# A transformer block on one core: identity transposes at the start, later weight loads, a sixth lo tile, normalisation ahead of its transposes

## The chip, the core and the metric

The kernel runs on one core of a Trainium2 chip. It is written in Bass with the Tile framework. The metric is device time in microseconds (us) of one execution; lower is better. The engines are TensorE (PE: matmuls and transposes; PEld is its weight load), VectorE (DVE), ScalarE (ACT), GpSimd (POOL) and SyncE (SP, which issues most DMAs). Each engine executes its own instructions in order. The instructions that the kernel pins with `tc.keep_in_program_order` (in the code through `mm`, `transpose` and `act`) stay in the order of the program; the compiler may place the others earlier, by its own estimate of when they are ready. SP's DMAs and ScalarE's normalisations are among these others.

## What is computed

Two sequences of 2048 tokens with 512 features go through one transformer block with adaptive layer norm; 16 heads of 32 features, a hidden layer of 2048, all in float32. The reference, cut:

```python
mod = silu(condition) @ Wada + bada
sh_a, sc_a, gt_a, sh_m, sc_m, gt_m = split(mod, 6, axis=1)
xm = (layernorm(x) * g1 + be1) * (1 + sc_a) + sh_a
q, k, v = split(xm @ Wqkv)                       # heads of 32
scores = causal(q @ k.T * 32 ** -0.5)
x = x + gt_a * (softmax(scores) @ v @ Wproj + bproj)
xm = (layernorm(x) * g2 + be2) * (1 + sc_m) + sh_m
x = x + gt_m * (gelu(xm @ W1 + b1) @ W2 + b2)
```

## The kernel before

The two sequences (rows 0 and 1) go through a QKV stage and an attention stage one after the other: QKV 0, attention 0, projection 0 with the preparation of row 1, QKV 1, attention 1, projection 1, and then one MLP stage for both.

**The opening.** ScalarE's queue loads the small vectors into `rows`. SP loads the first 512 tokens (`load_x(0)`, four tiles of 128 x 512), two 512-column pieces of Wada (`load_wada(0, 1)`, eight DMAs of 256 KB), then the weights of q and k (`load_w`) and of v (`load_wv`). TensorE transposes `rows` into `ps_c` (L1290), from which the column vectors `cols` are copied. For the four token tiles `stats` gives mean and variance on VectorE, and `inv_std` the reciprocal deviation `rstd1` and the `shift1`, with ScalarE's square root between. `norm(0, 0, True)` normalises two tiles on ScalarE (L866) and transposes them with TensorE (`ps_xt`, L212). Then `modulation(0)` multiplies silu(condition) with Wada (`ps_mod`); `norm(0, 1, True)` does the other two tiles; `columns()` adds the bias to `ps_mod` (L1314) and turns the result into columns (`ps_modt`); `scale_shift` makes the factors `a1` and `c1`, and `modulate` writes the modulated, transposed tokens `xmT` from the banks of `ps_xt`.

**A QKV stage** (`Qkv.run`) has four groups of 512 tokens. A group has six units: four of q and k (`keys_and_queries`) and two of v (`values`). A unit is a Strassen product in seven steps of four matmul instructions each, 0.87 us a step. Group 0 of row 0 begins with a plain unit instead (`plain`, L998), which counts as seven steps. After each step `tick` runs, with the step number `n` in the group `g`. It is the schedule that the change edits: at n = 3 the tokens of the next group are loaded, at n = 18 and 28 `norm` does the halves of the next group, statistics first, at 36, 38, 40 the token sums are made, and from n = 7 of group 1 on a plan (`row.count`) inserts score matmuls of the coming attention (`s`), whose maxima VectorE takes (`mx`, L481 and L476). These share two score banks in PSUM (tag "s") with `ps_mod` and `ps_modt`.

**q and k tiles.** The results are gathered in a `lo` tile (five buffers in row 0, six in row 1), rounded into a `hi` tile (three buffers), `lo` becomes the difference, and SP stores both to DRAM (`stored`, L924). A buffer is free again when its store has landed. `key_loads` and `query_loads` bring back what attention needs (L323, L348).

**Prepared weights.** The same stage prepares the MLP weights. `Pieces.plan(f, room, load, start)` loads a piece of W1 or W2 at a tick `load` (SP, L1119 and L1128), adds its Strassen sums on GpSimd from tick `start` on (L1140), and GpSimd's queue stores them to DRAM. Ticks run through the stage: group 0 of row 0 has 41, each further group 42. The rooms are tiles that are not yet in use: parts of the values `vv`, two key tiles and two query tiles (`spare_q`, taken from the four buffers of `qst`). `load_wada(2, 5)` runs at step 7 of group 0, `modulation(g + 1)` at step 10 of groups 1 and 2, `columns()` at step 14, and there `load_wada(3, 4)` in group 1. `mr` holds the bias rows for that in a tile of its own.

**Row 1.** While projection 0 runs, `between(n)` makes the statistics of row 1's first group and runs `norm` at n = 5 and 8. After that QKV 1 is as QKV 0, without Wada and modulation.

## Time and profile before

| | us |
|---|---|
| median of 3 runs (2357.98 to 2359.51) | 2358.91 |
| the profiled execution | 2359.31 |
| its span, first to last instruction | 2357.5 |
| TensorE busy / VectorE / GpSimd / ScalarE | 2311.3 / 1433.9 / 1120.0 / 1008.0 |

TensorE's busy time by stage:

| stretch, us | stage | length | TensorE busy | granted clock |
|---|---|---|---|---|
| 0 to 20 | opening | 20 | 9.25 | 0.98 |
| 20 to 214 | QKV 0 | 194 | 182.92 | 0.98 |
| 214 to 780 | attention 0 | 566 | 561.35 | 1.00 |
| 780 to 816 | projection 0 | 36 | 34.38 | 1.00 |
| 816 to 996 | QKV 1 | 180 | 175.13 | 0.99 |
| 996 to 1560 | attention 1, projection 1 | 564 | 559.30 | 1.00 |
| 1560 to 2357 | MLP | 797 | 788.94 | 1.00 |

How the page is read: a group is a line, an engine, an operation and the tiles it writes and reads; then its count, its busy time and the mean of one instruction, and the idle time of that engine just before, with what ended it. Idle time of an engine that does not set the end costs nothing. Matmuls are pipelined and their ends are modelled, so that a busy TensorE need not be at its peak. The granted clock is the share of full speed that TensorE was given, by the profiler's records; before the first record it is shown as 1.00.

### The profile page before, as it was taken

What the parts mean: (1) busy time and instruction counts of PE and PEld (TensorE: products, weight loads), DVE (VectorE), ACT (ScalarE), POOL (GpSimd) and SP (SyncE); (2) the same over time, 40 slices, a digit from 0 to 9 for tenths busy, and PEclk for the clock granted to TensorE, in tenths of its full rate; (3) what the DMA queues carried; (4) which work ended last, traced back from release to release, by engine and by line L of the source; (5) the groups of instructions that cost most, each with busy time, mean ns of one, the idle gap of its engine ahead of it and who ended that gap; (6) DMA issues with size and microseconds to landing.
All of it is one profiled execution on the core that took longest, in us unless ns stands there. A gap on an engine that the chain in (4) does not pass through costs nothing.

```text
span 2357.5 us, 34284 instructions
## 1 busy us (share of the span) xinstructions
PE 2311.3 (98%) x12033; PEld 1403.5 (60%) x12033; DVE 1433.9 (61%) x2960; ACT 1008.0 (43%) x1952; POOL 1120.0 (48%) x1261
## 2 busy tenths in 40 slices
PE   7999999999999999999999999999999999999998
PEld 5877555555554488855555555444585486487477
DVE  4567666666666666776666666653473374365356
ACT  4434555555555244355555555603323322332321
POOL 7152997978793593289887997460000000000000
PEclk9999999999999999999999999999999999999999
DMA  9887133231232797532324113273254254353433
GB/s 303 262 260 194 38 81 74 64 82 46 79 110 91 256 304 247 140 84 59 82 64 99 38 45 121 78 252 111 94 171 148 89 180 143 115 167 128 135 124 130
DMA packets 160518, 311.64 MB, mean 132 GB/s; under 512 B 16544, under 2 KB 48844, under 8 KB 158552
## 3 DMA queue, kind: packets, MB, share of 16 engines
q1 hardware_dynamic: 155488, 285.53, 40.0%
q0 software_dynamic: 4480, 23.36, 2.6%
q8 instruction: 95, 1.56, 0.3%
q14 instruction: 79, 0.65, 0.1%
q10 hardware_dynamic: 376, 0.55, 0.1%
HBM read 229.95 MB, written 87.29 MB: 135 GB/s over the span
## 4 chain that ended last, share of the span: by engine, by line
PE 92%; DVE 3%; DMA 2%; POOL 1%; ACT 1%; issue 1%; SPq 0%; DVEq 0%; POOLq 0%; ACTq 0%
PE ps_a L204 24%; PE st L204 20%; PE ps_b L204 12%; PE o L204 11%; PE s L204 10%; PE ps_c L204 6%; PE sm L204 4%; PE ps_o L204 3%; PE ps_xt L212 1%; POOL ee L634 1%; DVE mx L481 1%; PE ps_o L212 1%; DVE junk L476 0%; DMA x<-in_x_dram 0%; DMA q<-lo 0%
## 5 line engine op out<-in xcount | busy, mean ns | idle before, releaser
L606 ACT ACTIVATE e<-st 128x512 f32<-128x512 f32 (+1 forms) x1152 | 573.4, 578 | 429.4 <-PE st L204 369.4
L634 POOL TENSOR_TENSOR ee<-ee,e 128x512 f32<-128x512 f32 x424 | 529.3, 1290 | 4.5 <-ACT e L606 4.2
L481 DVE TENSOR_REDUCE mx<-s 128x1 f32<-128x512 f32 x604 | 407.4, 687 | 194.5 <-PE s L204 193.2
L204 PE MATMUL s<-kst,qst 128*128 128x512 f32 (+3 forms) x1032 | 418.6, 409 | 9.3 <-DVE mx L481 7.8
L204 PE MATMUL st<-qst,kst 128*128 128x512 f32 (+3 forms) x1280 | 409.4, 387 | 0.0
L204 PE MATMUL ps_a<-sum,w 128*128 128x256 f32 (+1 forms) x1088 | 346.6, 454 | 0.0
L204 PE MATMUL o<-e,vv 128*32 128x512 f32 (+3 forms) x2560 | 300.5, 538 | 2.0 <-POOL e L612 2.0
L204 PEld LDWEIGHTS st<-qst,kst 128*128 128x128 f32 x1280 | 227.4, 188 | 94.1 <-issue 62.1
L476 DVE CUSTOM_DVE_ANT_0 junk<-s,causal 128x512 bf16<-128x512 f32 (+3 forms) x428 | 208.6, 487 | 106.7 <-PE s L204 99.2
L204 PEld LDWEIGHTS ps_a<-sum,w 128*128 128x128 f32 x1088 | 206.3, 190 | 109.8 <-issue 91.4
L204 PEld LDWEIGHTS s<-kst,qst 128*128 128x128 f32 x1032 | 194.8, 189 | 124.7 <-DVE mx L481 62.0
L634 POOL TENSOR_TENSOR ee<-e 128x512 f32<-128x512 f32 x168 | 210.5, 1287 | 102.3 <-ACT e L606 100.0
L612 POOL TENSOR_SCALAR_AFFINE_SELECT e<-e 128x128 f32<-128x128 f32 (+1 forms) x384 | 122.6, 360 | 82.6 <-ACT e L606 79.8
L204 PE MATMUL st<-fold,sel 32*128 32x512 f32 (+1 forms) x1152 | 148.6, 481 | 0.4
L1590 DVE TENSOR_TENSOR h<-c,ps_b 128x512 f32<-128x512 f32 x32 | 22.0, 687 | 202.4 <-PE ps_b L204 202.4
L204 PEld LDWEIGHTS st<-fold,sel 32*128 32x128 f32 x1152 | 59.1, 181 | 143.1 <-ACT e L606 86.6
L204 PEld LDWEIGHTS o<-e,vv 128*32 128x32 f32 x2560 | 61.3, 108 | 101.8 <-issue 80.1
L204 PE MATMUL ps_b<-sum,w 128*128 128x256 f32 (+1 forms) x384 | 120.6, 450 | 0.0
L1764 ACT ACTIVATE h<-h,cols 128x512 f32<-128x512 f32 x96 | 69.2, 722 | 118.6 <-DVE h L1590 118.6
L481 DVE TENSOR_REDUCE mx<-st 128x1 f32<-128x512 f32 x164 | 112.7, 687 | 4.2 <-PE st L204 2.4
L959 POOL TENSOR_TENSOR lo<-lo,hi 128x512 fp32r<-128x512 f32 x32 | 40.7, 1273 | 134.2 <-ACT hi L957 113.9
L204 PEld LDWEIGHTS ps_b<-sum,w 128*128 128x128 f32 x384 | 73.0, 190 | 37.2 <-issue 30.6
(205 smaller groups left out, 3108.0 us busy)
## 6 DMA issues: line engine op xcount, KB each, us to landing
kst<-k SPq DMA_DIRECT2D x128, 256.0 KB
qst<-q SPq DMA_DIRECT2D x128, 256.0 KB
w<-w1d SPq DMA_DIRECT2D x32, 896.0 KB
w<-w2d SPq DMA_DIRECT2D x28, 1024.0 KB
w<-w2d SPq DMA_DIRECT2D x28, 768.0 KB
q<-hi SPq DMA_DIRECT2D x32, 256.0 KB
q<-lo SPq DMA_DIRECT2D x32, 256.0 KB
k<-hi SPq DMA_DIRECT2D x32, 256.0 KB
```

Of the source, the lines that this page charges most:

```text
L204: return tc.keep_in_program_order(nc.tensor.matmul(*args, **kw))
L212: return tc.keep_in_program_order(nc.tensor.transpose(dst, src, ident[:n, :n]))
L476: nc.vector.tensor_tensor_reduce(junk[:, :w], s[:, :w], causal[:, QB - w :], 1.0, MASKED, ALU.add, ALU.max, m,)
L481: nc.vector.tensor_reduce(m, s[:, :w], axis=AX.X, op=ALU.max)
L606: act(nc.scalar.activation(e[:, :w], sts[h][:, :w], AF.Exp))
L612: nc.gpsimd.affine_select(d, d, pattern=[[0, len(tiles)], [1, P]], compare_op=ALU.is_ge, fill=0.0, base=0, channel_multiplier=-1,)
L634: act(engine.tensor_tensor(dst, x, y, ALU.add))
L959: engine.tensor_tensor(lo, d, hi.bitcast(F32), ALU.subtract)
L1590: act(nc.vector.tensor_tensor(dst, x, y, ALU.add))
L1764: nc.scalar.activation(d, ps, AF.Gelu, bias=col(r_b1 + half * HF + f, 1))
```

## The change

- After the weight loads are issued, TensorE does 34 transposes of the identity into a score bank `ps_w` that nobody reads. They stand ahead of the transpose of `rows`.
- The normalisation leaves `norm` and becomes `normal`. In the opening it runs on VectorE, as (x - mean) * rstd, for all four tiles, and both halves are transposed before `modulation(0)`. In the groups it stays on ScalarE and runs at n = 14 and 24, with the statistics of the group at 14; the transposes stay at 18 and 28. In projection 0 it runs at n = 4 and 7, with the transposes at 5 and 8.
- `lo` has six buffers in both rows. `mr` moves into the end of a spare query tile (the last 512 of 2048 columns; the piece there uses the first 896).
- `load_wada(2, 5)` moves from step 7 to 24 of group 0; `modulation` and `columns` from steps 10 and 14 to 3 and 7 of groups 1 and 2, and with the latter `load_wada(3, 4)`.
- The pieces of W1 and W2 are loaded and summed at later ticks.

```diff
+        def normal(self, g, j, early=False):
+            b = self.row.b
+            if j == 0 and g > b:
+                for t in range(MTT):
+                    self.stats(g, t)
+            for t in (2 * j, 2 * j + 1):
+                n, xt = b * NT + g * MTT + t, self.xts[g][t]
+                if early:
+                    nc.vector.tensor_scalar(
+                        xt, xt, mv1[:, n, 0:1], rstd1[:, n : n + 1],
+                        ALU.subtract, ALU.mult,
+                    )
+                else:
+                    nc.scalar.activation(
+                        xt, xt, AF.Identity,
+                        bias=shift1[:, n : n + 1], scale=rstd1[:, n : n + 1],
+                    )
         def norm(self, g, j, share=False):
             if j == 0:
-                if g > b:
-                    for t in range(MTT):
-                        self.stats(g, t)
                 self.xmT[g] = self.qp.tile([P, C, MT], F32, tag="xmT", ...)
-            for n, xt in enumerate(xts, n0):
-                nc.scalar.activation(
-                    xt, xt, AF.Identity,
-                    bias=shift1[:, n : n + 1], scale=rstd1[:, n : n + 1],
-                )
...
-            return hp.tile([P, MT], F32R, tag="lo", name="lo", bufs=5 + self.row.b)
+            return hp.tile([P, MT], F32R, tag="lo", name="lo", bufs=6)
...
+                        if n in (14, 24):
+                            self.normal(g + 1, n // 24)
                         if n in (18, 28):
                             self.norm(g + 1, n // 28)()
...
+        spare_q = [row.old_queries().rearrange("p h q -> p (h q)") for _ in range(2)]
...
-                mr = wp.tile([P, D], F32, tag="mr", name="mr")
+                mr = spare_q[0][:, HC * QB - D :]
...
+        ps_w = ps_sp.tile([P, QB], F32, tag="s", name="ps_w")
+        for _ in range(34):
+            transpose(ps_w[:, :P], ident)
         ps_c = ps_mm.tile([P, n_rows], F32, tag="mm", name="ps_c")
         transpose(ps_c, rows)
...
-        halves = [qkv.norm(0, 0, True)]
+        for j in range(2):
+            qkv.normal(0, j, True)
+        halves = [qkv.norm(0, j, True) for j in range(2)]
...
         columns = modulation(0)
-        halves.append(qkv.norm(0, 1, True))
         columns()
...
-            if g == 0 and n == 7:
+            if g == 0 and n == 24:
                 load_wada(2, 5)
-            elif g in (1, 2) and n == 10:
+            elif g in (1, 2) and n == 3:
                 qkv.columns = modulation(g + 1)
-            elif g in (1, 2) and n == 14:
+            elif g in (1, 2) and n == 7:
                 qkv.columns()
...
-        pieces.plan(FC // 2, room_2, 5, 17)
+        pieces.plan(FC // 2, room_2, 16, 27)
...
-            (room_v, 4, 38), (room_k, 58, 68), (room_q, 62, 73), (room_k, 84, 93),
-            (room_q, 88, 98), (room_k, 108, 116), (room_q, 112, 121), (room_w, 101, 126),
+            (room_v, 34, 46), (room_k, 64, 73), (room_q, 68, 78), (room_k, 88, 97),
+            (room_q, 93, 102), (room_k, 110, 118), (room_q, 114, 122), (room_w, 104, 126),
...
+            if n in (4, 7):
+                qkv.normal(0, n // 7)
             if n in (5, 8):
                 qkv.norm(0, n // 8)()
```

More of the change, by code (lines that the diff above doesn't have):

```diff
@@ L1381, in dit_block_kernel @@
         pieces = Pieces()
-        spare_q = [row.old_queries().rearrange("p h q -> p (h q)") for _ in range(2)]
         spare_k = [row.key_room(q) for q in (2, 3)]
```

## The prediction

> **What bounds the kernel now.** I read the page first. TensorE is busy 98% of the span and 92% of the chain that ended last, so only what gives TensorE idle time, or a half clock, can move the end. I then asked for the waits of TensorE over the whole span, for stretches of 0.5 and 2 us through the two QKV stages (row 0: 19 to 214 us, row 1: 816 to 995 us), and for the chain and timeline around each idle stretch. The change touches nothing of the attention, projection and MLP matmuls, so the question is how much idle time lies in those stages.

> The opening, from the chain of waits in order of time (start, us, what):

> ```profile
> 8.18 1.53 ACT x L866 x2
> 9.75 1.75 PE ps_xt L212 x7
> 11.51 3.85 PE ps_mod L204 x16
> 15.36 1.24 PE ps_xt L212 x8
> 16.60 0.80 PE ps_modt L204 x8
> 18.12 1.90 DVE xmT L267 x4
> ```

> The first tokens are normalised on ScalarE, eight transposes follow, the modulation matmul `ps_mod`, eight more transposes, the small `ps_modt`, then the modulated tokens; the first projection matmul starts at 19.17. Seven transposes take 1.75 us here (250 ns each), while eight take 0.87 us at 54.92 (109 ns each), and `ps_mod` takes 3.85 us here against 1.86 at 77.48: TensorE runs at half speed, though the clock column shows 1.00 until 19.0.

> The granted clock by stretches (busy us of PE, PEld, DVE, ACT, POOL, then PEclk):

> ```profile
> 19.00:19.50 0.50, 0.33 (x1) 0.33 (x2) 0.50 (x3) 0.50 (x2) 0.48 (x2) 0.69 1.11 352
> 19.50:20.00 0.50, 0.50 (x1) 0.17 (x1) 0.50 (x3) 0.50 (x2) 0.50 (x1) 0.50 1.08 346
> ...
> 22.50:23.00 0.50, 0.50 (x2) 0.19 (x1) 0.50 (x1) 0.00 (x0) 0.50 (x2) 0.89 0.92 324
> ```

> 0.69 and 0.89 put the half-clock stretch at 19.2 to 22.6: 3.4 us, so 1.7 us of TensorE work lost. The 2 us stretches show three more of the same length, at 49.9, 128.4 and 920.3, each just after an idle stretch. So an idle stretch of 2 us or more costs itself and 1.7 us more. The three, from the timeline (start, us, what, in brackets the idle time before and its releaser):

> ```profile
> 33.81 5.21 SPq L1280 DMA_DIRECT2D vv<-in_L_cond_Wada_dram  x8
> 47.51 0.62 ACT L957 CAST hi<-lo 128x512 fp32r<-128x512 f32 x1 [1.89 <-DMA q<-hi]
> 48.68 1.10 PE L204 MATMUL ps_b<-xmT,wqk 128*128 128x256 f32 x4 [3.49 <-ACT lo L952]
> ```

> ```profile
> 116.11 3.92 SPq L1119 DMA_DIRECT2D kst<-in_L_cond_W_dram  x4
> 120.12 2.10 SPq L816 DMA_DIRECT2D x<-in_x_dram  x4
> 124.13 0.69 DVE L216 BATCH_NORM_STATS2 stat<-x 128x6 f32<-128x512 f32 x1 [2.17 <-DMA x<-in_x_dram]
> 127.29 0.44 PE L204 MATMUL s<-kst,qst 128*128 128x384 f32 x1 [1.80 <-DVE mx L481]
> ```

> ```profile
> 872.93 0.33 PE L212 MATMUL ps_xt<-ident,x 128*128 128x128 f32 x1 [0.88 <-ACT x L866]
> ...
> 918.60 0.33 PE L212 MATMUL ps_xt<-ident,x 128*128 128x128 f32 x1 [1.70 <-ACT x L866]
> ```

> First: SP spends 5.2 us issuing Wada, the stores of q queue behind it (the chain has `q<-lo` from 40.64 for 7.49 us), and ScalarE waits for its `hi` and `lo` tiles. Second: the tokens of group 3 are issued behind a W1 load, VectorE waits for them with the score maxima behind it, and one of the two score banks is still held by `ps_mod`. Third: transposes wait for their normalisation.

> **The change, part by part.**

> Opening. The 34 identity transposes can start when the identity is made (1.41+0.29 = 1.70). At 109 ns they end at 5.4, at 250 ns at 10.2. Normalising moves to VectorE and needs no shift: after the reciprocal (7.95) four tensor_scalar of 128x512. The row of that form (L248, in the MLP) is 512 ns at least, 863 median beside GpSimd work; GpSimd is idle from 5.4 to 17.4, so I take 512. First tokens at 8.5, against 9.0; all sixteen transposes end at 10.7 (four per 512 ns). Silu's table load no longer queues between normalisations. `ps_mod` then waits for Wada: its last chunk was waited for until 13.11 (0.57 us behind a DMA), and the load order before it is the same. With the clock up the last quarter takes 0.5 us, end 13.6 against 15.36; the addition 0.69 and eight `ps_modt` at 0.80 follow, then 1.7 us to the first projection as now (17.43 to 19.17): 17.2 against 19.17, **−2.0 us**. Bounds: if the clock stays up through the projection too, 1.7 more (−3.7); if the transposes never raise it, 34 end at 10.2, sixteen more at 250 ns at 14.5 with `ps_c`, `ps_mod` 3.85 at 18.4, first projection at 22.0: +2.8. I take −2.0, with a half-clock stretch after it as now: TensorE still idles about 2 us before the first projection.

> Does an identity transpose count as work for the clock? By the trace, the stretch 2350.5 to 2353.9 holds 0.8 us of matmul and transposes beside it, and the clock stayed at 1.00, while 46.5 to 49.9, with 1.2 us of matmul, was followed by half clock: they seem to count. Against it, 9.0 to 12.4, mostly transposes with TensorE busy for 3.12 of 3.4 us, did not raise it: `ps_mod` ran on at half speed. [...]

> Wada (2,5) from step 7 to 24, the W2 and W1 pieces from 5 and 4 to 16 and 34, and `lo` from five tiles to six. This clears SP and the DMA queue between 26 and 40 us, and the first write of unit 3 meets a tile whose store was issued at 26, not at 40. It removes 3.49 us and the 1.7 after it: **−5.2**. Row 1 has six `lo` tiles and no Wada load, and its first group (816 to 860) shows no such wait. Bounds −5.2 and 0.

> Where does it go? From step 24 to step 14 of group 1 about 26 us pass, which at 390 GB/s (40 to 66 us ran at 390 to 428) carry 10.1 MB. Wada 2.1, W1 0.5, W2/W1 stores 4.0, q/k stores 2.1, tokens 1.0 and, with its load moved from step 14 to 7, the second Wada 2.1 make 11.8: 4 us too much. Late first are the k stores of group 1 behind the second Wada's 5.2 us on SP; their `hi` tile is wanted about 10 steps (8.7 us) later. Bounds 0 and a stall as before, 5.2. I take **+3**, nearer that row, as the sum is over.

> Modulation from steps 10 and 14 to 3 and 7 of groups 1 and 2. Scores run from step 7 on, so `ps_mod` no longer holds a score bank beside them. Tokens are loaded at step 3 and the W1 pieces go from step 1 of group 2 (tick 84) to step 5 (88), so the tokens are ahead of them by 3.92 us of SP. This answers 1.80+0.25+0.48 of idle time and 1.7 of half clock, 4.2; two of its three causes go, I take **−3.1**, bounds −4.2 and 0.

> `normal` at steps 14 and 24 ahead of transposes at 18 and 28, with the statistics, in both rows; in the projection one step ahead. Four steps are 3.5 us or more; the waits are 0.88+0.38 in one group of row 1 and 1.70+0.38+1.7 in another: **−5.1**, bounds −5.1 and 0. No instruction is added; ScalarE (9 of 20 us busy there) and VectorE (14 of 20) hold it. What queues behind: an unfinished token load now meets VectorE and ScalarE four steps sooner, with maxima and `lo` evictions behind. Issue to last statistics is 71.70 to 79.9, 8.2 us; steps 3 to 14 give 11 x 0.87 = 9.6. The cover is 1.4 us.

> At nothing: `mr` in the spare query tile (same memset and wait on GpSimd), the later W1 sums (GpSimd is 48% busy), one more table load wait at 28 to 31 us as now.

> Sum: −2.0 −5.2 +3.0 −3.1 −5.1 = −12.4. The profiled execution took 2359.3 (span 2357.5); the runs' median is 2358.9. So **2347 us**.

> **The rivals.** (a) The warm-up does not do what it says: opening +2.8 in place of −2.0, 2359.3−7.6 = 2351.7. For: the half speed at 9 to 12 us with transposes running. Against: the stretch at the end. (b) The moved transfers stall group 1 of row 0 in place of group 0: +5.2 in place of +3 and the group 3 tokens still late (0 for −3.1): −2.0−5.2+5.2−5.1 = −7.1, 2352; with one of row 1's two waits kept, 2355 or more. For: the 11.8 MB. Against: only stores with slack are late. (c) Slower: tokens land after step 14, in-order VectorE and ScalarE stop there, and each such group costs what group 3 costs now, 4.2. The gains at 128, 872 and 918 fall, −4.2 remains. Six groups have the moved step; from two late groups on the change loses, with three it is −4.2+12.6 = +8.4, 2367.7. For: 1.4 us of cover and a full queue. Against: after the token load at 903.72 the DMA share is 0.82 to 0.88, not full.

> **How the numbers follow.** Forecast 0.53, (a) 0.22, (b) 0.15, (c) 0.10. All bounds at their good end give −19.1, 2340; 2359 leaves out (c) and little else. 0.2% (4.7 us) is what a measurement can tell. Faster: 0.53 + 0.20 of (a) + 0.05 of (b) = 0.78; same: 0.02+0.10 = 0.12; slower 0.10. Without (b)'s poor half and (c) the range would be 2340 to 2354.

> **What would show it.** Right: first projection matmul near 17; transposes of tokens near 109 ns; no wait of `ps_b` for ScalarE near 46; no half clock near 128 and 920; the row 1 stage (815.7 to 995.6 now, 179.9 us) about 5 us shorter. Wrong: token transposes at 250 ns and a first projection after 19 (a); a wait of ScalarE for `q<-hi`, `k<-hi` or `lo` stores between 65 and 90 us (b); VectorE's statistics waiting for `x<-in_x_dram` with TensorE idle in several groups (c).

## The result, and the profile after

The change made the kernel slightly slower: 2363.89 us median of 22 runs against 2359.45 us of 22 runs of the kernel before, a ratio of 1.0018 with a 95% interval of 1.0010 to 1.0026, so 2.4 to 6.1 us. The forecast was 2347, with a range of 2340 to 2359; the result lies above it. The profiled execution of after took 2364.2 (span 2362.5, TensorE busy 2316.3).

How far a mark of after stands from the same mark of before, in the one profiled execution of each, shows the place (us):

| mark | before | after | after less before |
|---|---|---|---|
| first projection matmul | 19.17 | 18.90 | -0.3 |
| first Strassen unit (`ps_a`) | 27.83 | 25.87 | -2.0 |
| attention 0, first matmul | 214.96 | 220.78 | +5.8 |
| QKV 1, first unit | 815.65 | 821.90 | +6.3 |
| attention 1, first matmul | 995.56 | 999.71 | +4.2 |
| MLP, first transposes | 1560.01 | 1564.44 | +4.4 |

So the opening and QKV 1 each gained 2, and QKV 0 lost 7.8 between its first Strassen unit and its end. What TensorE waited for most in the first 215 us of after (in total, times, longest):

```profile
PE ps_a L204 <- POOL wv L846: 8.5, 1, 8.5
PE s L204 <- DVE mx L476: 3.3, 3, 2.7
PE ps_xt L212 <- ACT x L869: 2.0, 2, 1.8
PE ps_a L204 <- DVE lo L982: 1.9, 1, 1.9
```

The wait of `ps_b` for `lo` at 45 to 49 us is gone, as forecast. In its place stands one of 8.5 us. The profile puts it down to GpSimd's value weight sums, but this matmul reads neither `wv` nor anything made from it. The timelines from 23 to 37 us tell more (start, us, what, in brackets the idle time before and its releaser). VectorE of after:

```profile
23.26 0.69 DVE L216 BATCH_NORM_STATS2 stat<-x 128x6 f32<-128x512 f32 x1 [2.92 <-DMA x<-in_x_dram]
26.42 3.08 DVE L1379 COPY pick<-pickc 128x512 f32<-128x512 f32 x1
...
30.69 3.96 DVE L901 TENSOR_TENSOR xmT<-xmT 128x512 f32<-128x512 f32 x1
34.66 0.66 DVE L216 BATCH_NORM_STATS2 stat<-x 128x6 f32<-128x512 f32 x1
```

GpSimd of after:

```profile
26.45 2.77 POOL L841 TENSOR_TENSOR wqk<-wqk 128x256 f32<-128x256 f32 x4
...
30.41 5.37 POOL L846 TENSOR_TENSOR wv<-wv 128x512 f32<-128x512 f32 x4
```

ScalarE and then TensorE of after:

```profile
35.57 0.30 ACT L222 ACTIVATE rstd<-mv,eps 128x4 f32<-128x4 f32 x1 [7.61 <-DVE mv L219]
35.78 0.36 ACT L963 ACTIVATE lo<-ps_a 128x256 f32<-128x256 f32 x1
```

```profile
26.73 1.03 PE L204 MATMUL ps_b<-t,wqk 128*128 128x256 f32 x4
36.24 2.05 PE L204 MATMUL ps_a<-t,wqk 128*128 128x256 f32 x4 [8.48 <-POOL wv L846]
```

Read backwards: TensorE goes on at 36.24, 0.1 us after ScalarE has evicted `ps_a` into `lo`. ScalarE could not evict before, because `rstd` of group 1 stood ahead in its queue and waited 7.61 us for the last mean and variance from VectorE. VectorE was late because it had waited 2.92 us for group 1's tokens ahead of `pick` and `xmT`, a copy and a sum of group 0, and because these two then took 3.08 and 3.96 us beside GpSimd's sums. In before they took 0.94 and 0.84, although they lay beside GpSimd's sums there too. GpSimd, then VectorE of before:

```profile
19.31 10.48 POOL L841 TENSOR_TENSOR wqk<-wqk 128x256 f32<-128x256 f32 x12
```

```profile
24.14 0.94 DVE L1361 COPY pick<-pickc 128x512 f32<-128x512 f32 x1
25.01 0.68 DVE L216 BATCH_NORM_STATS2 stat<-x 128x6 f32<-128x512 f32 x1
...
26.87 0.84 DVE L890 TENSOR_TENSOR xmT<-xmT 128x512 f32<-128x512 f32 x1
```

There GpSimd's sums took 0.87 us each, in after 0.69, so in before it was GpSimd's sums that took longer. What decides which of the two engines takes longer is not shown.

Group 1's statistics are issued at step 14 by the new program text and at 18 by the old one, but in both queues the compiler has placed them near the beginning of group 0. In before they stand behind `pick`; in after the first of them stands ahead of it. By the clock records the clock was at half from 30.6 to 40.9 us; TensorE worked for 4.6 us of that, so 2.3 were lost to it. The windows (busy us of PE, PEld, DVE, ACT, POOL, then PEclk) show both halves of the loss, the idle one and the slow one:

```profile
32.00:36.00 4.00, 0.00 (x0) 0.00 (x0) 3.96 (x5) 0.43 (x2) 3.92 (x4) 0.50 0.56 179
36.50:41.00 4.50, 4.50 (x12) 3.58 (x12) 0.42 (x1) 3.31 (x5) 2.06 (x3) 0.51 0.65 178
```

A second new stretch lies in group 1, where the tokens of group 2 come late. SP, VectorE and TensorE of after:

```profile
77.60 4.35 SPq L816 DMA_DIRECT2D x<-in_x_dram  x4
84.40 6.68 SPq L1294 DMA_DIRECT2D vv<-in_L_cond_Wada_dram  x8
```

```profile
85.33 0.69 DVE L216 BATCH_NORM_STATS2 stat<-x 128x6 f32<-128x512 f32 x1 [6.67 <-DMA x<-in_x_dram]
```

```profile
87.35 0.33 PE L204 MATMUL s<-kst,qst 128*128 128x128 f32 x1 [2.70 <-DVE mx L476]
89.55 3.78 PE L204 MATMUL ps_a<-t,wqk 128*128 128x256 f32 x8 [1.87 <-DVE lo L982]
```

The mechanism is that of rival (c): tokens come late, VectorE stops in order, and score maxima and `lo` stand behind it; that makes 2.70 + 1.87 us idle, and 3.0 us more are lost at half clock from 88.7 to 95.5. The cause is another: the two experiments below that keep the later loads but have the statistics back at step 18 show the same stretch, so the moved loads make it and not the earlier step.

In group 3 VectorE does not wait for its tokens any more, and the score wait of before at 127 us is down to 0.29. In its place TensorE waits for the normalisation, which it did not do there in before, with 3.4 us of half clock as before:

```profile
143.43 0.47 PE L212 MATMUL ps_xt<-ident,x 128*128 128x128 f32 x1 [1.81 <-ACT x L869]
```

### The profile page after: what moved, and what is told of

It reads as the page before. It is cut to its first block, busy times and chain, and to the rows that moved or that the text cites. A ratio compares the mean times of both kernels' runs of the same rounds, so it can differ in the third digit from the quotient of the medians.

```text
span 2362.5 us, 34358 instructions
## 1 busy us (share of the span) xinstructions
PE 2316.3 (98%) x12067; PEld 1409.6 (60%) x12067; DVE 1437.2 (61%) x2964; ACT 1005.3 (43%) x1948; POOL 1117.3 (47%) x1261
## 4 chain that ended last, share of the span: by engine, by line
PE 90%; DVE 3%; DMA 2%; POOL 2%; issue 1%; ACT 1%; SPq 0%; POOLq 0%; DVEq 0%; ACTq 0%
PE ps_a L204 24%; PE st L204 20%; PE ps_b L204 12%; PE o L204 11%; PE s L204 10%; PE ps_c L204 6%; PE sm L204 4%; PE ps_o L204 2%; PE ps_xt L212 1%; DVE mx L481 1%; POOL ee L634 1%; DVE junk L476 1%; PE ps_o L212 1%; DMA x1d<-xt 0%; DMA x<-in_x_dram 0%
## 5 line engine op out<-in xcount | busy, mean ns | idle before, releaser
L481 DVE TENSOR_REDUCE mx<-s 128x1 f32<-128x512 f32 x604 | 407.6, 687 | 196.3 <-PE s L204 195.0
L204 PE MATMUL s<-kst,qst 128*128 128x512 f32 (+3 forms) x1032 | 418.5, 409 | 11.0 <-DVE mx L481 7.1
L204 PE MATMUL st<-qst,kst 128*128 128x512 f32 (+3 forms) x1280 | 409.4, 387 | 0.0
L204 PE MATMUL ps_a<-sum,w 128*128 128x256 f32 (+1 forms) x1088 | 346.6, 454 | 0.0
L204 PE MATMUL o<-e,vv 128*32 128x512 f32 (+3 forms) x2560 | 300.5, 538 | 1.9 <-POOL e L612 1.9
L204 PEld LDWEIGHTS st<-qst,kst 128*128 128x128 f32 x1280 | 227.4, 188 | 94.2 <-issue 62.0
L204 PEld LDWEIGHTS ps_a<-sum,w 128*128 128x128 f32 x1088 | 206.3, 190 | 109.8 <-issue 91.4
L204 PEld LDWEIGHTS s<-kst,qst 128*128 128x128 f32 x1032 | 194.7, 189 | 124.1 <-DVE mx L481 59.3
L204 PE MATMUL st<-fold,sel 32*128 32x512 f32 (+1 forms) x1152 | 148.5, 480 | 0.4
L204 PEld LDWEIGHTS st<-fold,sel 32*128 32x128 f32 x1152 | 59.2, 181 | 143.2 <-ACT e L606 86.6
L204 PEld LDWEIGHTS o<-e,vv 128*32 128x32 f32 x2560 | 61.5, 108 | 101.5 <-issue 79.4
L204 PE MATMUL ps_b<-sum,w 128*128 128x256 f32 (+1 forms) x384 | 120.6, 450 | 0.0
L1783 ACT ACTIVATE h<-h,cols 128x512 f32<-128x512 f32 x96 | 69.3, 722 | 120.4 <-DVE h L1609 120.4
L481 DVE TENSOR_REDUCE mx<-st 128x1 f32<-128x512 f32 x164 | 112.7, 687 | 4.2 <-PE st L204 1.8
L204 PEld LDWEIGHTS ps_b<-sum,w 128*128 128x128 f32 x384 | 73.0, 190 | 37.2 <-issue 30.6
```

The source lines that it names most:

```text
L204: return tc.keep_in_program_order(nc.tensor.matmul(*args, **kw))
L481: nc.vector.tensor_reduce(m, s[:, :w], axis=AX.X, op=ALU.max)
L1783: nc.scalar.activation(d, ps, AF.Gelu, bias=col(r_b1 + half * HF + f, 1))
```

## The experiments

Ratios are to runs of the kernel before on the same chip in the same batch, with their 95% intervals. In the five batches the median of before lay at 2357.8 to 2360.1, and its single runs spread over 2350.7 to 2369.4, so a ratio near 1 says more than a median. A profile is of one execution, and some were the slowest of their runs; it shows where time goes rather than the price.

**The place of group 1's statistics.** They are kept in program order, nothing else is changed:

```diff
-                    self.stats(g, t)
+                    self.stats(g, t, b == 0 and g == 1)
```

> The changed kernel with one difference: the statistics of group 1 in row 0 are kept in program order, so that they stand in VectorE's queue behind the pick copy, the token sums and the first lo tiles, and the deviation rstd behind the first evictions in ScalarE's queue. Theory A (queue order: the statistics and rstd, placed early by the compiler, stand in front of lo evictions): the idle stretch of TensorE at 27.8 to 36.2 us (8.5 us) and the half clock behind it (10.2 us, at most 5.1 lost) go, the time falls by 8 to 13 from 2363.9, to 2351 to 2356. Theory B (GpSimd's work on the weight sums alone slows VectorE's copies and sums, whatever the order): pick and the token sum still take 3 to 4 us each, lo comes late all the same, and the time falls by less than 4, to 2360 or more.

2353.68, ratio 0.9974 (0.9962 to 0.9986), which is 0.44% or 10.4 us below the changed kernel. The wait of 8.5 is gone. `pick` takes 1.40 and the sum `xmT` 1.06, both now earlier (21.6 and 25.1 us), ahead of GpSimd's value weight sums; theory A holds. The second stretch is gone too, since SP issues the tokens of group 2 at 71.6 and not at 77.6 us: near 85 TensorE waits for no more than 0.45. So 10.4 us is what the pin gives for both stretches together, less the new waits that it brings (1.9 for `vv` at 65, with half clock behind it). What is left of the first is a shorter wait, since the statistics now come somewhat late for their transposes; the sum `xmT` on VectorE, then TensorE:

```profile
25.14 1.06 DVE L901 TENSOR_TENSOR xmT<-xmT 128x512 f32<-128x512 f32 x1 [0.40 <-PE ps_qk L204]
```

```profile
40.27 0.33 PE L212 MATMUL ps_xt<-ident,x 128*128 128x128 f32 x1 [3.09 <-ACT x L869]
```

**The opening alone** (loads, modulation, group normalisation and `lo` buffers as before):

```diff
-            if g == 0 and n == 24:
+            if g == 0 and n == 7:
                 load_wada(2, 5)
...
-                        if n in (14, 24):
-                            self.normal(g + 1, n // 24)
+                        if n in (18, 28):
+                            self.normal(g + 1, n // 28)
```

> The opening alone: identity transposes, VectorE normalising all four tiles and both halves transposed ahead of the modulation (with the bias rows in the spare query tile); loads, modulation, normalisation in the groups and lo buffers as before. Theory A (the opening alone makes the compiler place the statistics of group 1 early): the new idle stretch near 28 to 36 us is here too, the first projection gains about 0.3 and the full clock 1.7, and the time is 2362 to 2370 (before 2359.4). Theory C (the later loads or the earlier normalisation make that stretch): it is absent, and the time is 2359.4 - 2.0, some 2357.

2360.52, ratio 1.0000 (0.9990 to 1.0011). The place was right, the time below what theory A gave. The stretch is here, so the opening alone makes it:

```profile
PE ps_a L204 <- POOL wv L846: 7.0, 1, 7.0
PE ps_b L204 <- ACT lo L963: 3.5, 3, 1.4
```

But the wait for `lo` stores at 45 to 49 us has shrunk from 3.5 to one of 2.1 at 53 and one of 0.9 at 56: while TensorE stood still at 28 to 36, SP and the stores went on. So the new stretch covers part of the old one; that this is why the time does not rise is argued.

**The opening alone, with the statistics pinned.** The same one line added to the last kernel:

> The opening alone (which took as long as the kernel before, ratio 1.0000) with the statistics of group 1 pinned. Theory A (the place of the statistics took what the opening gave): 2.0 from the forecast's opening show, 2357 and 0.9985 to 0.9995, or more if the early statistics cost 7 to 10 as in the changed kernel and leave no wait in their place, down to 0.9960. If the statistics hide behind the stretch at 45 to 49 us, which stands here, the ratio stays near 1.0000.

2358.22, 0.9997 (0.9985 to 1.0008). With the old load steps pinning gives nothing: the transposes of group 1 now wait, and TensorE stands as long as it did:

```profile
PE ps_xt L212 <- ACT x L869: 8.9, 3, 8.2
```

**The identity transposes, taken out**, first of the changed kernel, then of the pinned one:

```diff
-        for _ in range(34):
-            transpose(ps_w[:, :P], ident)
```

> The changed kernel without the 34 identity transposes, all else kept. In it the compiler puts the pick copy ahead of the statistics of group 1 again. Theory A (the identity transposes push the first tokens later in the compiler's estimate, and so the statistics in front of pick and the token sums): the idle stretch at 28 to 36 us shrinks or goes, the opening runs at half clock again (token transposes 250 ns, first projection 1 to 4 us later than 18.9), and the time falls to 2355 to 2361. Theory B (the stretch comes from elsewhere): the stretch stays and the slower opening adds, 2364 to 2368. In both, if identity transposes raise the granted clock, the first full clock is later than 6.8 us here.

2359.86, 1.0007 (0.9992 to 1.0021). The compiler puts `pick` ahead of the statistics again, and the 8.5 us stretch is gone. So VectorE's early normalisation does not move the statistics without the identity transposes; whether these would do it alone was not run. Presumably they are work in the compiler's own estimate, so that group 0's sums look later to it and group 1's tokens look ready; that part is argued and not shown. The time is not told apart from that of the changed kernel by the intervals: the second stretch stays (3.79 and 1.87 us idle, half clock from 81.4 to 88.2), and the slower opening adds. The clock side, TensorE in the changed kernel (PEld is its weight load) and then without identity transposes:

```profile
1.75 6.35 PE L212 MATMUL ps_w<-ident 128*128 128x128 f32 x34 [1.75 <-POOL ident masks.py:199]
8.73 2.35 PE L212 MATMUL ps_xt<-ident,x 128*128 128x128 f32 x16 [0.44 <-DVE x L864]
9.19 1.66 PEld L212 LDWEIGHTS ps_xt<-ident,x 128*128 128x128 f32 x15 [0.31 <-DVE x L864]
```

```profile
8.21 3.92 PE L212 MATMUL ps_xt<-ident,x 128*128 128x128 f32 x16 [1.14 <-DVE x L864]
```

245 ns a token transpose without, 147 with them, where the first two still wait for the normalisation and the weight loads of the rest follow at 111 ns. The first full clock comes at 6.8 us with, at 13.1 without: here identity transposes raised the clock. The first projection does not clearly gain by that: it starts at 18.28 without them, and at 17.8 to 18.9 in the profiles of the kernels with them.

> The kernel with the pinned statistics (0.9974 of before) without the identity transposes; the queue order of VectorE behind the opening is the same, so the difference is their own. Forecast of the prediction (they raise the clock ahead of the tokens' transposes and of ps_mod; its two ends lie 4.8 apart): first Strassen unit 1 to 3 us later than 26.7, ratio to before 0.9980 to 0.9995. If the clock is up by then anyway, or half clock comes back behind the opening in both, the ratio stays at 0.9970 to 0.9980.

2356.18, 0.9985 (0.9975 to 0.9996), against 0.9974 with them. The first Strassen unit starts at 27.90 against 26.66. The point estimates differ by 2.6 us, near the forecast, but the two intervals overlap.

**The later loads alone** (with modulation, six `lo` tiles and `mr`; opening and normalisation as before):

> The later loads, the earlier modulation, the sixth lo tile and the bias rows in the spare query tile alone; opening and normalisation as before. Theory A: no idle stretch at 28 to 36; the stretch of before at 45 to 49 (3.5 and 1.7 of half clock) is gone; the tokens of group 2 come late behind the moved loads if these are to blame for the stretch at 85 to 91. With that 2354 to 2359, without it 2351 to 2354. Theory C (the loads make the stretch at 28 to 36): it is here, 2362 or more.

2360.65, 0.9999 (0.9987 to 1.0011). No stretch at 28 to 36, and the one at 45 to 49 is gone, but nothing is left of that:

```profile
PE ps_xt L212 <- ACT x L866: 6.2, 6, 3.3
PE s L204 <- DVE mx L476: 4.7, 1, 4.7
```

The 4.7 us is the second stretch of after, followed by 1.7 for `lo`: SP issues the tokens of group 2 at 71.5 behind a W1 load, and the clock is at half from 80.7 to 87.5. The moved loads alone make it. That it takes back what the wait at 45 to 49 gave is argued from this profile.

**The old load steps, with the statistics pinned** (pieces, Wada and modulation back in the kernel of the first experiment):

> The kernel with the pinned statistics of group 1 (2353.7), with the loads, the modulation and the pieces back at their old steps; lo keeps six tiles. Theory L (the later loads take more than they give, by moving GpSimd's W2 sums onto the token sums of group 2 and the tokens behind a W1 load): the waits at 64 to 66 and 134 us shrink and the time falls, 2349 to 2353. Theory M (the later loads pay what the forecast says, 5.2 at 45 to 49 us): that stretch returns, 2357 to 2360.

2359.70, 1.0001 (0.9991 to 1.0010), against 0.9974: in this setting the later loads are worth 0.27%, 6.4 us. The number is that of theory M, its place is not: the wait of `ps_b` for `lo` at 45 to 49 does not return, but the transposes of group 1 wait 5.9 us in place of 3.1.

**Normalisation of row 0 back at steps 18 and 28:**

> The changed kernel with statistics and normalisation of row 0's groups back at steps 18 and 28, next to their transposes; row 1 keeps steps 14 and 24. Theory A (the stretch at 28 to 36 comes from the opening's queue order): it stays, the queue order of group 1 being the same, and only the waits near 88 and 143 change: 2358 to 2364. Theory D (the earlier step of the normalisation is the cause of all three new stretches): all three go, 2350 or less.

2364.88, 1.0020 (1.0008 to 1.0032): no difference from the changed kernel. The queue order of group 1 is the same in both, and its wait is there (7.1 in place of 8.5). So is the second stretch: VectorE waits 6.31 us for the tokens of group 2, TensorE 2.35 and 1.87 behind it. The earlier step makes neither.

**Row 1's earlier normalisation alone**, in the kernel before:

```diff
-                            self.norm(g + 1, n // 28)()
+                        if n in ((18, 28) if row.b == 0 else (14, 24)):
+                            self.normal(g + 1, n >= 24)
```

> The kernel before with one step of the change: in row 1 the statistics and the normalisation of the groups at steps 14 and 24, and in the projection at 4 and 7, ahead of their transposes; row 0 as before. Forecast of the prediction: the waits of transposes for the normalisation (1.26 at 872 us, 2.08 and 1.7 of half clock at 918 us) go, -5.1, to 2354. Theory S (these waits and the half clock come and go from run to run, and the step is worth what the stage of the changed kernel showed): -2 or less, 2357 to 2359, with the stage between the first unit and the first attention matmul of row 1 177 to 178 us long against 179.05.

2355.35, 0.9982 (0.9968 to 0.9995): 4.2 us by the ratio, 1.2 to 7.5 by its interval. It holds the forecast of 5.1 and theory S's 2 alike. The stage is 176.1 us long against 179.05, both counted from the second step of its first unit (816.51 in before). The waits of the transposes in row 1 come to 1.0 us in three pieces, none above 0.4; a wait of 1.2 for score maxima is new, and after has it too.

**GpSimd beside VectorE.** In the changed kernel the value weight sums and the last four weight sums of q and k move to VectorE, later:

```diff
-            if (g, n) == (0, 7):
-                for k in range(4):
-                    qkv.weight_sum(nc.gpsimd, k, slice(0, P))
+            if g == 0 and 12 <= n < 16:
+                qkv.value_weight_sum(nc.vector, n - 12)
+            elif g == 0 and 16 <= n < 20:
+                qkv.weight_sum(nc.vector, n - 16, slice(0, P))
...
-        qkv.value_weight_sums()
```

> The changed kernel (statistics of group 1 early, as in it) with the four value weight sums and the last four weight sums of q and k on VectorE, at steps 12 to 19, in place of GpSimd, so that GpSimd is idle from about 29 us. Theory P (a copy or sum of VectorE makes no headway beside back-to-back GpSimd sums): the token sum xmT takes under 1.2 us in place of 3.96, and the idle stretch falls from 8.5 to 5 to 6. Theory Q (only the order and the waits for the tokens count): xmT begins later but the stretch keeps its 8 to 9. Pick lies beside the q and k sums in both and keeps some 3 us.

2362.02, 1.0005 (0.9993 to 1.0018). The sum beside which GpSimd is now idle, and the wait of TensorE:

```profile
30.45 0.67 DVE L906 TENSOR_TENSOR xmT<-xmT 128x512 f32<-128x512 f32 x1
```

```profile
32.71 2.04 PE L204 MATMUL ps_a<-t,wqk 128*128 128x256 f32 x4 [3.71 <-issue]
```

0.67 in place of 3.96, 3.7 in place of 8.5, more than expected. `pick`, still beside the sums of q and k, keeps 3.08. So 3.3 us of the wait (3.96 less 0.67) are the sum `xmT` beside GpSimd. The rest of the fall is mostly that the first unit of after came earlier: the opening alone, which starts it at 27.09 as this kernel does (27.11), waits 7.0. What remains is order, `pick` and the tokens' arrival. Theory P's number for this sum, under 1.2 us, came true; that VectorE makes no headway at all beside GpSimd's sums is not shown by it.

**The tokens of groups 2 and 3 asked for earlier**, with all statistics of row 0 pinned; then those of group 3 alone:

```diff
+                        if n == 30 and g + 2 < NG and row.b == 0:
+                            self.load_x(g + 2)
```

> The changed kernel with the statistics of all groups of row 0 kept in program order, and the tokens of groups 2 and 3 loaded at step 30 of the group before, when their tiles come free, in place of step 3. Rival (c) of the prediction (late tokens stop VectorE and ScalarE at step 14): the waits of VectorE for x go, with them the idle stretches at 64 to 66 and 134 us and their half clock, 2347 to 2351. If those stretches come from GpSimd's sums beside VectorE's and not from the tokens, the time stays within 2 of 2353.7.

> The kernel with the pinned statistics (2353.7), with the tokens of group 3 of row 0 loaded at step 30 of group 1 and their statistics pinned as well. Rival (c) (tokens too late for step 14, so that the transposes wait): TensorE's wait of 1.8 for x at 134 us and the half clock of 3.4 behind it go, -3.5, 2350. If the wait has another cause, the time stays within 2 of 2353.7.

2356.98, 0.9988 (0.9977 to 0.9998), and 2356.41, 0.9988 (0.9976 to 0.9999). Both missed, and the tokens of group 3 do not come earlier: SP issues them at 121.1 and 120.4 us, still behind a store of `k`, against 119.2 in the pinned kernel (those of group 2 move from 71.6 to 68.0 in the first). Nor does the pinned kernel wait for them: its wait at 134 is one of transposes for the normalisation. It stays (1.71 and 2.67 against 1.81), only without half clock behind it. So what late tokens of group 3 cost was not tested. In both the token sums of the group boundary, which in the pinned kernel take 1.06, 3.32 and 2.56, take 3.75, 2.45 and 1.07, and 3.34, 2.46 and 1.07, and waits of group 1's transposes remain (2.1 and 3.2 the longest).

**The W2 pieces at their old steps 5 and 17**, in the pinned kernel, so that GpSimd's sums end before that boundary; then together with the early tokens of group 3:

> The kernel with the pinned statistics (2353.7), with the W2 pieces alone back at steps 5 and 17, so that GpSimd's W2 sums end before the token sums of group 1 are made. Theory P (VectorE makes no headway beside GpSimd's sums): the token sums there take 0.7 to 1.2 us in place of 1.06, 3.32 and 2.56, TensorE's wait of 1.9 for vv at 65.5 and the half clock behind it go, 2349 to 2351. Against it (the W2 loads were moved for a reason): SP's loads of W2 push the first stores of q and k back and the stretch at 45 to 49 returns, 2355 to 2359.

> Both of the last two at once: if both causes hold and are separate, -7 from 2353.7, 2347; if the transfers collide, 2350 to 2355.

2353.10, 0.9972 (0.9960 to 0.9984), and 2352.73, 0.9970 (0.9959 to 0.9982). The token sums take 0.69 each and the wait for `vv` at 65 is gone, as theory P forecast, but the time is that of the pinned kernel: TensorE waits longer at 40 us (3.78 against 3.09), with 6.8 us of half clock there, where the pinned kernel has 3.4 at 66. Removing one stretch here lengthens its neighbour.

**Group 1's statistics at step 9**, pinned, with the W2 pieces at their old steps; then with the sums of GpSimd on VectorE as well:

```diff
-                        if n in (14, 24):
+                        if n in ((9, 24) if row.b == 0 and g == 0 else (14, 24)):
```

> The kernel with pinned statistics and the W2 pieces at steps 5 and 17 (0.9972), with the statistics and normalisation of group 1 at step 9 in place of 14. If the transposes of group 1 wait near 40 us because the statistics stand too late now, that wait (3.8) and its half clock (1.7 to 3.4 lost) go: 0.9950 to 0.9960 of before, some 2347 to 2350. If the statistics at step 9 stand in front of lo evictions again and hold TensorE, the ratio stays at 0.9970 or rises.

> The kernel with the statistics of group 1 at step 9 (0.9965 of before), with the four value weight sums and the last four of q and k on VectorE at steps 12 to 19 in place of GpSimd. Theory P (VectorE makes no headway beside GpSimd's back-to-back sums): the 128x4 shift takes under 0.5 us in place of 4.54, TensorE's wait of 3.0 at 35.8 goes, with its half clock, and the time falls by 2 to 5 to some 2347, 0.9945 to 0.9958. Otherwise shift keeps several us, or the added 4 us of VectorE work hold lo evictions later in group 0, and the ratio is 0.9965 or more.

2351.18, 0.9965 (0.9954 to 0.9977), and 2350.97, 0.9963 (0.9951 to 0.9975): the two lowest of this study, below both kernels, and not told apart from one another. In the first a VectorE operation of four elements a partition stands beside GpSimd's value weight sums; in the second GpSimd does not make these, and only a W2 sum (30.78 to 32.04) lies beside it:

```profile
30.52 4.54 DVE L224 SCALAR_TENSOR_TENSOR shift<-mv,rstd 128x4 f32<-128x4 f32 x1
```

```profile
31.75 0.31 DVE L224 SCALAR_TENSOR_TENSOR shift<-mv,rstd 128x4 f32<-128x4 f32 x1
```

The wait of 3.0 behind it went as expected, the time did not: GpSimd begins the W2 sums at 30.8, and the sums that VectorE took over lie beside them (2.86 us for two of 128x512, 1.75 for one, 2.95 for two of 128x256), with a new wait of 1.85 for `lo` at 42.

## Why the prediction was wrong, point by point

**The step that failed** is a line that was put down at nothing: "one more table load wait at 28 to 31 us as now". That is the place where group 1's statistics meet group 0. In before TensorE waits there for 0.89 us:

```profile
30.61 1.10 PE L204 MATMUL ps_a<-t,wqk 128*128 128x256 f32 x4 [0.89 <-POOL wqk L841]
```

After the change it waits 8.48 us, with 4.6 us of work at half clock behind. The statistics kept in program order, and nothing else, bring the kernel from 1.0018 to 0.9974 of before, 10.4 us, the second stretch included. With the old load steps the pin gives nothing (0.9997 against 1.0000), so it has this price only beside the later loads. The opening's −2.0 was reckoned from what the engines do there; what the added transposes do to the compiler's order behind them was not priced, although the text before the prediction said that the compiler may place such instructions earlier. That the order goes back without these transposes is shown; why the compiler chooses it is not.

**The rivals.** (c) had the right mechanism: statistics early in an in-order queue, with evictions behind them. Its place and cause were wrong. It priced late tokens at step 14 at 4.2 a group and needed two such groups; that happened once in after (84 to 91 us), through the moved loads and not the step, and the larger case was in group 0, set by the compiler. (a) is refuted: with the warm-up the full clock came at 6.8 us, without it at 13.1. But the first projection does not clearly come earlier by it, and in the profiles of ten of the thirteen kernels with identity transposes half clock was back at 16.5 to 19.1 us (there `ps_qk` took 8.54 to 10.12 us, in the other three 7.13). (b) is seen: alone, the moved loads stall group 1 of row 0 by 4.7 and 1.7 us.

**The terms.**
- Opening, −2.0: the first Strassen unit came 2.0 earlier in that profile, by luck more than by the way forecast. Wada's last part was waited for until 14.18 and not 13.11, so the first projection gained only 0.3. The other 1.7 is full clock through `ps_qk` (7.13 against 8.82), which the text had only among its bounds and which three of the thirteen kernels show. The old opening itself gives 25.78, 27.83 and 28.12 for that unit in three profiles, in which `ps_qk` starts at 18.81, 19.17 and 19.68 and takes 7.13, 8.82 and 8.61.
- Later loads, −5.2, +3 and, for the modulation, −3.1, together −5.3: nothing when alone (at most 3.1), 6.4 with the statistics pinned. In after the new stretch at 28 to 36 gives the stores the same time, as the opening alone shows.
- Of these, +3 was too small: the stall that it stands for took 2.70 + 1.87 us idle and 3.0 at half clock in after, 7.6 against an upper bound of 5.2. The sum behind it also took a row wrongly: from 40 to 66 us the queue moved 240 to 428 GB/s, 372 in the mean and not 390 or more, so that the excess was 5.6 us and not 4.
- And −3.1: the wait for group 3's tokens went, but transposes that wait as long (1.81 + 0.23) with the same half clock took its place in after.
- Row 1, −5.1: 4.2 with an interval that holds 5.1.
- The moved loads were taken to be issued at their new ticks. In after SP issues the first W2 loads at 20.34 and two pieces of Wada at 23.98 and 30.55: the compiler placed them early here as well.

- Slips of the sums that change nothing in the outcome: the row 1 terms add to 5.0, the good ends to −18.2 (2341), the opening as printed to 16.8; the 0.48 in the modulation term is a gap of the weight loads, where TensorE itself waited 0.36.

The worths of the parts do not add up to the whole: the 10.4 of the pin and the time of the loads alone both contain the second stretch. In the two profiles TensorE's longer waits from the first Strassen unit to attention 0 come to 10.9 us in before and 16.3 in after, and half clock took 3.4 and 7.0; together after is 9.0 worse, near the 7.8 that it lost there.

**Open:** why the compiler moves the statistics, and what late tokens of group 3 cost. The second stretch of after was not undone by itself in the changed kernel.

## What to carry to other kernels

Where a compiler orders a queue by its own estimate, an edit that adds work on one engine can reorder the others; look at the new order of each in-order queue behind the edit before a cost is put at nothing, and pin the instructions that wait for a DMA. A wait that the profile puts on an engine whose output the waiting instruction does not read should be followed back through what frees its bank, here ScalarE's eviction and VectorE behind that. Where idle stretches follow each other closely, the price of one is not what its removal gives: the experiments that removed one or two gave from nothing to 10 us.

## What was not expected of the hardware

**VectorE beside GpSimd.** Operations of VectorE took several times their length beside back-to-back GpSimd sums: the sum `xmT` took 0.67 us with GpSimd idle and 3.96 in after with it busy, and a 128x4 operation took 4.54 where it took 0.31 without the value weight sums beside it. So in these profiles four elements a partition (4.54) took no less than 512 (3.96). It is no fixed price: in before the same 128x4 operation beside the value weight sums took 0.55, and `pick` 0.94 where it took 3.08 in after. What sets the price is not shown.

**Transposes and the clock.** Whether identity transposes raise the clock was open before the run. 34 of them brought the full clock at 6.8 us in place of 13.1, and a token transpose took 147 ns in place of 245. In the profiles of the 13 kernels with them it comes first at 4.6 to 7.8 us, in those of the 5 without at 13.1 to 15.9.

**An idle stretch need not cost half clock.** The kernel with row 1's step alone has, in its profile, the wait for `lo` in row 0 that the kernel before has (3.24 us here, 3.49 there), and the clock stays up behind it and until the last 1.2 us of the span:

```profile
46.22 1.10 PE L204 MATMUL ps_b<-xmT,wqk 128*128 128x256 f32 x4 [3.24 <-ACT lo L963]
```

```profile
48.00:52.00 4.00, 4.00 (x24) 3.57 (x23) 0.84 (x2) 1.50 (x4) 3.98 (x7) 1.00 1.07 310
```
